# Both joins of a block's running sums in one burst of an attention kernel, instead of one in each of two

## The chip, the cores and the metric

The kernel runs on one core of one Trainium2 chip. The metric is the device time of one launch in microseconds (us): 1815.76 us, the median of three runs (1815.04 to 1822.94). The engines are named as in the profile: PE is TensorE's matmuls and PEld its weight loads, DVE is VectorE, ACT is ScalarE, POOL is GpSimd, SP is SyncE, which here issues DMAs.

## The reference, cut to what matters

```python
# x: (4, 512, 48, 48); 8 heads of d = 64 channels; t = 48 * 48 = 2304 tokens
hn  = group_norm(x, 32 groups) * scale + bias
qkv = einsum('oc,bchw->bohw', qkv_w, hn) + qkv_b        # then cast to float16
w   = softmax(einsum('bhct,bhcs->bhts', q * s, k * s), axis=-1)   # s = 64 ** -0.25
a   = einsum('bhts,bhcs->bhct', w, v)                   # float32
out = x + einsum('oc,bchw->bohw', proj_w, a) + proj_b
```

## The kernel before, in words

The attention is worked through in 16 pairs `g` of heads (4 images of 4 pairs; two heads side by side, 64 rows each). A pair's 2304 queries are cut into five blocks `j`: four of 512 queries and one of 256. So there are 80 blocks. For each block the 2304 keys are taken in bursts of three steps (`BURST = 3`); a block of 512 has six bursts, one of 256 has three. All bursts of all blocks stand in one list, `stream`, 432 entries long, and the loop over `n` at the end of `fast_path` goes through it. It writes every engine's queue by hand; no scheduler reorders it, and each engine works its own queue in order.

In the turn of burst `n` the loop writes, in this order:

- for a block whose last burst was `n - 3`: `add_up` (L1268), matmuls of the block's accumulator `acc` with a column of ones, which give the sums of the exponentials in the bank `sl`, and `rows` (L1284), DVE's copy of them out of the bank;
- `scores` of burst `n`: six matmuls (L1188) into three banks `ps`, and three exponentials on ACT (L1195) into the tile `p`;
- `add` of burst `n - 1`: on DVE, the burst's 128x3072 exponentials are added into `acc` (L1242). A block's first burst needs no addition, so the turn that handles it has none;
- `values` of burst `n - 2`: the matmuls `av<-p,v` (L1213), and, for a block's last burst, ACT's copy of the result to `avx` (L1222). The bank `av` is the one that `sl` takes over (`ps_av`, one buffer);
- `fill`: pieces of other work that are kept in the list `beside`: projections of q, k and v for later pairs and of the output for earlier ones (L840, L988, L717, L1092). A piece is a chain of matmuls into the one bank of `ps_w` and its evacuation on DVE (L868, L881, L727, L996, L1119). How many pieces a turn takes is set by a count of their costs and not by time;
- `join` at the end of the turn.

At a block's end `acc` holds three parts of 128x1024 (one for each step of a burst). `join(g, j, r)` adds part `r` to part 0 on DVE (L1247), so that `add_up` has one part to multiply by the ones. A block has two joins, `r = 1` and `r = 2`. With `e` the block's last burst, `r = 1` is written at the end of the turn `e + 1`, which also adds the exponentials of `e`, and `r = 2` at the end of the turn `e + 2`. The `add` of that turn is that of burst `e + 1`, the next block's first, so it adds nothing. `add_up` follows at the start of the turn `e + 3`. The last two blocks of the last pair don't join; 78 blocks do, with 156 joins.

POOL forms sums of x and of weights for the projections (L797, L775 to L778), multiplies `avx` by the inverse sums (L1337) and issues a DMA of the result (L1344).

Of the kernel before, what the change touches and what calls it, by code (L numbers as in the profile page):

```python
# [32 lines left out]
BURST = 3  # L33
# [434 lines left out]
def fast_path(  # L468
# [599 lines left out]
    def fetch(b, j):  # L1068

        o, n = QBLOCKS[j]  # L1070
        t = work.tile([P, NC, QB], F16, tag="attl", bufs=1, name=f"attl_{b}_{j}")
        pairs = NC - 1 if b == B - 1 else NC
        nc.sync.dma_start(
            t[:, :pairs, :n],
            atd[b].rearrange("(c p) t -> p c t", p=P)[:, :pairs, o : o + n],
        )
        fetched[b, j] = t
        fetch_at[b, j] = now[0]
# [89 lines left out]
    stream = []  # L1168
# [7 lines left out]
    def scores(u):  # L1176
        g, j, k, _ = u
        o, n = QBLOCKS[j]
        per = QB // n
        qt, kt = qk[g]  # L1180
        pt = ppool.tile([P, BURST, 2, QB], F16, tag="p", name=f"p_{g}_{j}_{k}")
        for r in range(BURST):
            ps = ps_s.tile([P, 2, QB], F32, tag="ps", name=f"ps_{g}_{j}_{k}_{r}")
            for a in range(per):
                i = (k * BURST + r) * per + a
                for h in range(2):
                    rows = slice(h * D, (h + 1) * D)
                    nc.tensor.matmul(  # L1188
                        ps[:, h, a * n : (a + 1) * n],
                        kt[rows, bass.ts(i, P)],  # L1190
                        qt[rows, o : o + n],
                        start=True,
                        stop=True,
                    )
            nc.scalar.activation(pt[:, r], ps, AF.Exp)  # L1195
        pts[u] = pt
# [27 lines left out]
    def add(u):  # L1224

        g, j, k, last = u
        pt = pts[u]
        if k == 0:
            acc[g, j] = [pt]
            return  # L1230
        if j >= NQ - 2 and g == NG - 1 and (last or j == NQ - 1):
            acc[g, j].append(pt)
            return
        before = acc[g, j][0]
        if k == 1:
            acc[g, j] = [
                work.tile(
                    [P, BURST, 2, QB], F16, tag="acc", bufs=1, name=f"acc_{g}_{j}"
                )
            ]  # L1240
        t = acc[g, j][0]
        nc.vector.tensor_tensor(t, before, pt, ALU.add)  # L1242

    def join(g, j, r):

        t = acc[g, j][0]
        nc.vector.tensor_tensor(t[:, 0], t[:, 0], t[:, r], ALU.add)  # L1247
        if r == BURST - 1:
            acc[g, j] = [t[:, :1]]

    def add_up(g, j, bank=None, more=False):


        o, n = QBLOCKS[j]
        per = QB // n
        sl = bank
        if bank is None:
            sl = ps_av.tile([P, QB], F32, tag="av", name=f"sl_{g}_{j}")
        steps = [
            (t, r, a)  # L1260
            for t in acc.pop((g, j))
            for r in range(t.shape[1])
            for a in range(per)
        ]
        for i, (t, r, a) in enumerate(steps):
            for h in range(2):
                lo = h * D
                nc.tensor.matmul(  # L1268
                    sl[lo : lo + D, :n],
                    ones16,  # L1270
                    t[:, r, h, a * n : (a + 1) * n],
                    start=(i == 0 and (g, j) not in open_sums),
                    stop=(i == len(steps) - 1 and not more),
                )
        if more:
            acc[g, j] = []
            open_sums.add((g, j))
        return sl

    def rows(g, j, sl):  # L1280

        o, n = QBLOCKS[j]
        sx = work.tile([P, QB], F32, tag="rows", name=f"slx_{g}_{j}")
        nc.vector.tensor_copy(sx[:, :n], sl[:, :n])  # L1284
        sm = small.tile([P, 2, QB // P], F32, tag="sums", name=f"sums_{g}_{j}")
        for h in range(2):
            nc.sync.dma_start(sm[:, h, : n // P], sx[h * D : h * D + 1, :n])
        sums[g, j] = sm
        return sx
# [9 lines left out]
    def check_sums(g, j):  # L1299
        n = QBLOCKS[j][1]  # L1300
        sm = sums[g, j][:, :, : n // P]
        ok = fine.rearrange("p (h i) -> p h i", h=2)[:, :, : n // P]
        for op, limit in ((ALU.is_ge, SUM_MIN), (ALU.is_le, SUM_MAX)):
            t = small.tile([P, 2, QB // P], F32, tag="in", name=f"in_{g}_{j}")
            t = t[:, :, : n // P]
            nc.gpsimd.tensor_scalar(t, sm, limit, None, op)  # L1306
            nc.gpsimd.tensor_tensor(ok, ok, t, ALU.mult)
# [278 lines left out]
    def pace(n):  # L1586

        rate, work = 0.0, 0.0
        for p in beside:
            us, need = p[0], p[6]  # L1590
            work += us
            left = min(need * per_pair, len(stream) - 4) - n
            rate = max(rate, work / max(left, 1))
        credit[0] = min(credit[0] + rate, 4.0)

    def fill(n, tasks_too=True):

        idle = beside and beside[0][4] and not beside[0][4]()  # L1600
        if ended(n - 1):
            room = 1.1 if idle else 0.0
        elif ended(n - BEHIND - 1):
            room = 1.1 if idle else 0.5
        else:
            room = 2.4 if idle else 0.8
        if tasks_too:
            do_tasks(room)
        closed = False
        while beside:  # L1610
            us, _, first, last, when, after = beside[0][:6]
            if after > n or (first and closed) or (when and not when()):
                break
            if us > 0.1 and credit[0] < us / 2:
                break
            issue()
            closed = closed or last
        if tasks_too:

            turn = next((p[7] for p in beside if len(p) > 7), None)  # L1620
            if turn is not None:
                prepare(turn + 1, 2)

    def wanted(g):

        while any(p[6] <= g for p in beside):
            while loads:
                loads.popleft()[1]()
            while tasks:
                tasks.popleft()[2]()  # L1630
            issue()
            credit[0] = max(credit[0], 0.0)

    ended = lambda n: 0 <= n < len(stream) and stream[n][3]
# [5 lines left out]
    def block_at(n):  # L1640

        return stream[n][:2] if ended(n) and n not in soon else None

    def joined(n):
        g, j = stream[n][:2]
        return not (g == NG - 1 and j >= NQ - 2)

    for n in range(end):
        now[0] = n
        while loads and loads[0][0] <= n:  # L1650
            loads.popleft()[1]()
        while fetches and fetches[0][0] <= n:
            fetch(*fetches.pop(0)[1:])
        summed = block_at(n - BEHIND - 1)
        pace(n)
        if summed:
            rows(*summed, add_up(*summed))
        wanted(stream[n][0])
        scores(stream[n])
        if n > 0:  # L1660
            add(stream[n - 1])
        if summed:

            fill(n)
        if n >= BEHIND:
            values(stream[n - BEHIND])
        if block_at(n - BEHIND - 2):
            check_sums(*block_at(n - BEHIND - 2))
        if block_at(n - BEHIND - 3):
            spread(*block_at(n - BEHIND - 3))  # L1670

        for late in (4, 5):
            found = block_at(n - BEHIND - late)
            if found and late == (4 if found[0] == NG - 1 else 5):
                divide(*found)
        if not summed:
            fill(n)

        if block_at(n - BEHIND - 2):
            invert(*block_at(n - BEHIND - 2))  # L1680
        for r in range(1, BURST):
            if ended(n - r) and joined(n - r):
                join(*stream[n - r][:2], r)
        if n - BEHIND in soon:
            g, j = stream[n - BEHIND][:2]
            sx = rows(g, j, add_up(g, j))
            if n - BEHIND == soon[1]:
                divide_here(g, j, sx, avx[g, j], nc.gpsimd)
        if n - BEHIND - 1 == soon[0]:
            check_sums(g, j)  # L1690
            invert(g, j)
        if n - BEHIND - 2 == soon[0]:
            spread(g, j)
            divide(g, j)
    g, b, j = NG - 1, B - 1, NQ - 1
    n = QBLOCKS[j][1]
# [99 lines left out]
```

## Time and profile before

| | |
|---|---|
| median of three runs | 1815.76 us (1815.04 to 1822.94) |
| the profiled execution | 1824.22 us, of which its instructions span 1822.5 us |
| busy: PE, DVE, ACT, POOL | 1603.8, 1284.5, 1341.7, 828.1 us |
| share of the span | 88%, 70%, 74%, 45% |
| mean granted clock of PE | 0.965 |
| joins (L1247) | 156, 163.2 us, mean 1046 ns |
| `sl` (L1268) | 192 matmuls, 35.3 us, and 151.6 us of idle PE before them |

In a row of groups stand line, engine, operation, the output and inputs by the program's names, the shapes and the count; behind the bar the busy time in us and the mean of one in ns; behind the second bar the idle time of that engine just before, and what ended it. A row of the timeline begins with start and length in us and ends with the idle time before it in brackets. A row of stretches begins with start, end and length, then gives for each engine the busy time and the count, and ends with PE's granted clock, the busy share of the DMA engines and GB/s; a `sum` row adds up such stretches.

### The profile page before, as it was taken

What the parts mean: (1) busy time and instruction counts of PE and PEld (TensorE: products, weight loads), DVE (VectorE), ACT (ScalarE), POOL (GpSimd) and SP (SyncE); (2) the same over time, 40 slices, a digit from 0 to 9 for tenths busy, and PEclk for the clock granted to TensorE, in tenths of its full rate; (3) what the DMA queues carried; (4) which work ended last, traced back from release to release, by engine and by line L of the source; (5) the groups of instructions that cost most, each with busy time, mean ns of one, the idle gap of its engine ahead of it and who ended that gap; (6) DMA issues with size and microseconds to landing.
All of it is one profiled execution on the core that took longest, in us unless ns stands there. A gap on an engine that the chain in (4) does not pass through costs nothing. (4 is left out here: it accounts for less than half of the span.)

```text
span 1822.5 us, 32530 instructions
## 1 busy us (share of the span) xinstructions
PE 1603.8 (88%) x12940; PEld 823.4 (45%) x12940; DVE 1284.5 (70%) x1553; ACT 1341.7 (74%) x1537; POOL 828.1 (45%) x1037
## 2 busy tenths in 40 slices
PE   6979898899989889989888999988989999889885
PEld 2634444344444444544444444444444444444443
DVE  5287677966767668796677767779777766776564
ACT  3267676677887778877777878787778778878783
POOL 2164652645664452264456445316456644552111
PEclk9999999999999999999999999999999999999898
DMA  6002020000100014610010002352100010223423
GB/s 202 1 10 62 17 72 15 20 19 17 30 22 21 16 63 134 170 42 23 22 30 23 19 15 65 102 183 60 24 27 23 25 22 17 68 72 118 134 86 106
DMA packets 108197, 100.07 MB, mean 55 GB/s; under 512 B 52372, under 2 KB 72084, under 8 KB 108036
## 3 DMA queue, kind: packets, MB, share of 16 engines
q1 hardware_dynamic: 102644, 87.20, 16.8%
q0 software_dynamic: 3488, 8.86, 1.5%
q8 instruction: 104, 1.70, 0.4%
q10 hardware_dynamic: 1904, 1.84, 0.3%
q14 instruction: 57, 0.47, 0.1%
HBM read 69.55 MB, written 28.01 MB: 54 GB/s over the span
## 5 line engine op out<-in xcount | busy, mean ns | idle before, releaser
L1195 ACT ACTIVATE p<-ps 128x1024 f16<-128x1024 f32 x1296 | 1232.1, 1026 | 439.1 <-PE ps L1188 370.3
L1242 DVE TENSOR_TENSOR acc<-acc,p 128x3072 f16<-128x3072 f16 x270 | 508.3, 1883 | 26.4 <-ACT p L1195 26.1
L1188 PE MATMUL ps<-q,k 64*128 64x512 f16 (+1 forms) x2880 | 372.7, 369 | 10.3 <-ACT p L1195 9.5
L1213 PE MATMUL av<-p,v 128*64 128x512 f16 (+1 forms) x2880 | 363.7, 366 | 0.1
L797 POOL TENSOR_TENSOR t<-x,t 128x256 f32<-128x256 f32 x240 | 205.0, 875 | 224.2 <-PE p L840 223.6
L988 PE MATMUL pv<-wqkv,x 128*64 128x256 f32 x2304 | 279.2, 391 | 6.4 <-DVE k L727 4.5
L1306 POOL TENSOR_SCALAR in<-sums 128x8 f32<-128x8 f32 (+1 forms) x158 | 89.4, 566 | 400.3 <-DMA sums<-slx 393.0
L1213 PEld LDWEIGHTS <-v 128*64 128x64 f16 x2880 | 132.8, 110 | 199.7 <-issue 151.1
L988 PEld LDWEIGHTS pv<-wqkv,x 128*64 128x64 f32 x2304 | 166.8, 141 | 104.7 <-issue 21.3
L1337 POOL TENSOR_TENSOR att<-avx,ib 128x512 f16<-128x512 f32 (+1 forms) x78 | 115.4, 1480 | 216.6 <-DMA ib<-row 197.7
L1188 PEld LDWEIGHTS <-k 64*128 64x128 f16 x2880 | 110.0, 96 | 220.2 <-issue 172.9
L840 PE MATMUL p<-t,s 128*64 128x256 f32 x1440 | 180.8, 388 | 3.5 <-DVE q L868 2.4
L1268 PE MATMUL sl<-acc,ones 128*64 128x512 f16 (+1 forms) x192 | 35.3, 393 | 151.6 <-DVE acc L1247 141.9
L1247 DVE TENSOR_TENSOR acc<-acc 128x1024 f16<-128x1024 f16 x156 | 163.2, 1046 | 0.7
L1242 DVE TENSOR_TENSOR acc<-p,p 128x3072 f16<-128x3072 f16 x79 | 150.0, 1899 | 0.0
L996 DVE TENSOR_TENSOR v<-pv,bv 128x512 f16<-128x512 f32 x72 | 49.7, 691 | 133.0 <-PE pv L988 133.0
L797 POOL TENSOR_TENSOR t<-x 128x256 f32<-128x256 f32 x120 | 130.4, 1107 | 22.6 <-PE p L840 22.4
L1092 PE MATMUL pr<-a,whi 128*128 128x512 f32 (+1 forms) x312 | 126.2, 412 | 10.0 <-ACT a L1064 4.8
L840 PEld LDWEIGHTS p<-t,s 128*64 128x64 f32 x1440 | 101.8, 140 | 66.9 <-issue 9.1
L797 POOL TENSOR_TENSOR t<-x,x 128x256 f32<-128x256 f32 x120 | 126.0, 1070 | 0.5 <-DVE x L668 0.4
L840 PE MATMUL p<-x,wqkv 128*64 128x256 f32 x960 | 121.7, 398 | 4.3 <-DVE v L996 2.8
L1092 PE MATMUL pr<-a,wlo 128*128 128x512 f32 (+1 forms) x312 | 117.5, 384 | 0.0
(90 smaller groups left out, 1326.5 us busy)
## 6 DMA issues: line engine op xcount, KB each, us to landing
r<-x_dram SPq DMA_DIRECT2D x72, 256.0 KB, 3.4
out_dram<-r SPq DMA_DIRECT2D x69, 256.0 KB, 2.3
ib<-row SPq DMA_DIRECT2D x126, 128.0 KB, 3.0
x<-x_dram SPq DMA_DIRECT2D x62, 256.0 KB, 5.1
attd<-att POOLq DMA_DIRECT2D x60, 128.0 KB, 2.2
attl<-attd SPq DMA_DIRECT2D x12, 512.0 KB, 4.2
x<-x_dram SPq DMA_DIRECT2D x16, 128.0 KB, 4.6
sums<-slx SPq DMA_DIRECT2D x128, 2.0 KB, 2.1
```

Of the source, the lines that this page charges most:

```text
L797: nc.gpsimd.tensor_tensor(t[:, c], ins[0][c], ins[1][c], ALU.subtract)
L840: nc.tensor.matmul(to[lo : lo + D, :], w[:, c, lo : lo + D], xs[c], start=(c == 0), stop=(c == 1),)
L988: nc.tensor.matmul(pw[0][lo : lo + D, a, :], hn[b, c, i * P // QB][:, at + lo : at + lo + D], wqkv[:, c, 2 * C + half * C // 2 :][:, : C / ...
L996: nc.vector.tensor_tensor(vv[b, half][:, i : i + 2, :], pw[0], bv[:, cols].unsqueeze(1).to_broadcast((P, 2, C // 2)), ALU.add,)
L1092: nc.tensor.matmul(ps[:, :n], w[:, c, bass.ts(m, P)], at32[b, j, c], start=(i == 0), stop=(i == len(steps) - 1),)
L1188: nc.tensor.matmul(ps[:, h, a * n : (a + 1) * n], kt[rows, bass.ts(i, P)], qt[rows, o : o + n], start=True, stop=True,)
L1195: nc.scalar.activation(pt[:, r], ps, AF.Exp)
L1213: nc.tensor.matmul(av[0][lo : lo + D, :n], vv[b, pr // 2][:, i, pr % 2 * P + lo : pr % 2 * P + lo + D], pt[:, r, h, a * n : (a + 1) * n], ...
L1242: nc.vector.tensor_tensor(t, before, pt, ALU.add)
L1247: nc.vector.tensor_tensor(t[:, 0], t[:, 0], t[:, r], ALU.add)
L1306: nc.gpsimd.tensor_scalar(t, sm, limit, None, op)
L1337: nc.gpsimd.tensor_tensor(to, avx.pop((g, j))[:, :n], ibs.pop((g, j))[:, :n], ALU.mult)
```

## The change

Both joins of a block are written at the end of the turn `e + 1`, the second directly behind the first; the turn `e + 2` has none. The sums are the same, in the same order.

```diff
         if block_at(n - BEHIND - 2):
             invert(*block_at(n - BEHIND - 2))
-        for r in range(1, BURST):
-            if ended(n - r) and joined(n - r):
-                join(*stream[n - r][:2], r)
+        if ended(n - 1) and joined(n - 1):
+            for r in range(1, BURST):
+                join(*stream[n - 1][:2], r)
         if n - BEHIND in soon:
```

On DVE's queue, around the end of pair 7's block 2, this stood before (`acc_2` is the block's accumulator, `t1q` and `q` the evacuation of the chain in the turn `e + 1`, `u2q` and `u3k` that in the turn `e + 2`, `slx` the copy of the sums):

```order
L1242 TENSOR_TENSOR acc_2_9043<-acc_2_9043,p_2_5_9139 128x3072
L881 TENSOR_SCALAR t1q_0_9202<-p_9_0_9193,bq 128x256
L868 SCALAR_TENSOR_TENSOR q_9191<-p_9_0_9193,t1q_0_9202 128x256
L1247 TENSOR_TENSOR acc_2_9043<-acc_2_9043 128x1024
L868 SCALAR_TENSOR_TENSOR u2q_0_9238<-p_9_0_9227,t1q_0_9202 128x256
L868 SCALAR_TENSOR_TENSOR u3k_0_9240<-p_9_0_9227,u2q_0_9238 128x256
L1247 TENSOR_TENSOR acc_2_9043<-acc_2_9043 128x1024
L1284 COPY slx_2_9246<-sl_2_9243 128x512
```

And this stands there now:

```order
L1242 TENSOR_TENSOR acc_2_9043<-acc_2_9043,p_2_5_9139 128x3072
L881 TENSOR_SCALAR t1q_0_9202<-p_9_0_9193,bq 128x256
L868 SCALAR_TENSOR_TENSOR q_9191<-p_9_0_9193,t1q_0_9202 128x256
L1247 TENSOR_TENSOR acc_2_9043<-acc_2_9043 128x1024 x2
L868 SCALAR_TENSOR_TENSOR u2q_0_9239<-p_9_0_9228,t1q_0_9202 128x256
L868 SCALAR_TENSOR_TENSOR u3k_0_9241<-p_9_0_9228,u2q_0_9239 128x256
L1284 COPY slx_2_9246<-sl_2_9243 128x512
```

The second join has moved ahead of the evacuation of the turn `e + 2`; nothing else changed places. On PE's queue the instructions stand in the same order as before. The chain in the turn `e + 3` (L840, behind `sl` and the six score matmuls) is where its waits differ; before, its rows and the two ahead of them were (`p` is the chain's bank, `ps` the scores; brackets name the semaphores waited for):

```order
L1188 LDWEIGHTS k_6424
L1188 MATMUL ps_3_2_2_9260<-q_6423,k_6424 128x512
L840 MATMUL p_9_0_9267<-t_9_0_8914,s_9_8906 64x256 [waits PE_49]
L840 MATMUL p_9_0_9267<-t_9_0_8914,s_9_8906 64x256 x3
L840 MATMUL p_9_0_9267<-x_2_0_6682,s_9_8909 64x256 x2
```

On PE's queue at the same place they now are:

```order
L1188 LDWEIGHTS k_6424
L1188 MATMUL ps_3_2_2_9260<-q_6423,k_6424 128x512
L840 MATMUL p_9_0_9267<-t_9_0_8914,s_9_8906 64x256 [waits DVE_49,PE_49]
L840 MATMUL p_9_0_9267<-t_9_0_8914,s_9_8906 64x256 x3
L840 MATMUL p_9_0_9267<-x_2_0_6683,s_9_8909 64x256 x2
```

The chain waits for DVE now, that is for the evacuation (`u3k`) of the bank that it writes; before, `sl` had already waited for a join that stood behind that evacuation.

## The prediction

> **What bounds the kernel now.** I read the waits of TensorE first, then the groups by line, then one block end on the timeline, then stretches behind every block end. In a row of waits stand the total, the number of waits and the longest.
>
> ```profile
> span 1822.5 us, 32530 instructions
> PE sl L1268 <- DVE acc L1247: 141.9, 69, 6.7
> PE sl L1268 <- ACT avx L1222: 9.7, 10, 2.2
> PE ps L1188 <- ACT p L1195: 9.5, 21, 0.5
> PE p L840 <- POOL t L797: 2.9, 1, 2.9
> ACT p L1195 <- PE ps L1188: 370.3, 300, 45.9
> L1247 DVE TENSOR_TENSOR acc<-acc 128x1024 f16<-128x1024 f16 x156 | 163.2, 1046 | 0.7
> ```
>
> TensorE hardly ever waits for ScalarE's exponentials (9.5 us) while ScalarE waits 370.3 us for scores, so TensorE sets the pace. Its one large wait is at `sl`, the matmuls that sum a block's accumulator: 141.9 us behind the joins (L1247). This block end (pair 7, block 2) shows why; the three fences are DVE, TensorE and ScalarE, with start, length and, in brackets, the idle time before.
>
> ```profile
> 916.67 0.42 DVE L868 SCALAR_TENSOR_TENSOR q<-p,t1q 128x256 f16<-128x256 f32 x1
> 917.01 0.68 DVE L1247 TENSOR_TENSOR acc<-acc 128x1024 f16<-128x1024 f16 x1
> 919.40 0.42 DVE L868 SCALAR_TENSOR_TENSOR u2q<-p,t1q 128x256 f32<-128x256 f32 x1 [1.71 <-PE p L840]
> 919.86 0.42 DVE L868 SCALAR_TENSOR_TENSOR u3k<-p,u2q 128x256 f32<-128x256 f32 x1
> 920.20 0.68 DVE L1247 TENSOR_TENSOR acc<-acc 128x1024 f16<-128x1024 f16 x1
> ```
>
> ```profile
> 917.46 1.89 PE L840 MATMUL p<-t,s 128*64 128x256 f32 x16
> 920.93 0.41 PE L1268 MATMUL sl<-acc,ones 128*64 128x512 f16 x2 [1.59 <-DVE acc L1247]
> 921.27 0.82 PE L1188 MATMUL ps<-q,k 64*128 64x512 f16 x6
> 924.55 0.82 PE L1188 MATMUL ps<-q,k 64*128 64x512 f16 x6
> ```
>
> ```profile
> 919.19 0.61 ACT L1222 COPY avx<-av 128x512 f32<-128x512 f32 x1
> 921.71 1.02 ACT L1195 ACTIVATE p<-ps 128x1024 f16<-128x1024 f32 x1 [1.91 <-PE ps L1188]
> ```
>
> The second join stands on DVE's queue behind `u2q` and `u3k`, the evacuation of the projection chain that TensorE itself has just finished at 919.35. So TensorE finishes the chain, DVE evacuates it for 0.8 us, joins for 0.68 us, and only then may `sl` start. DVE had been idle from 917.69 to 919.40: 1.71 us, in which a join of 0.68 us fits.
>
> **The change, part by part.** No arithmetic is added or removed: 78 second joins move one burst forward, to right behind the first join. SP's and POOL's queues issue the same instructions in the same order; the joins issue no DMA.
>
> (a) The wait at `sl`. With the second join at 917.70 to 918.38, what ends last is no longer DVE: it is `avx`, ScalarE's copy out of the one bank that `sl` takes over, ending at 919.80. I therefore cut out, for the 78 blocks that join, the stretch from the latest of three ends (TensorE's last matmul before `sl`; `avx`; first join plus the second join's length of this trace) to the start of `sl`. The first row is the sum of the whole waits of the 78, then that of the cut stretches.
>
> ```profile
> sum 149.85, PE 0.21 PEld 0.71 DVE 135.92 ACT 40.50 POOL 65.82; mean PE 0.00 PEld 0.01 DVE 1.74 ACT 0.52 POOL 0.84
> sum 88.20, PE 0.10 PEld 0.17 DVE 83.07 ACT 6.00 POOL 29.00; mean PE 0.00 PEld 0.00 DVE 1.20 ACT 0.09 POOL 0.42
> sum 100.03, PE 0.10 PEld 0.17 DVE 94.72 ACT 6.00 POOL 39.03; mean PE 0.00 PEld 0.00 DVE 1.37 ACT 0.09 POOL 0.57
> sum 83.10, PE 0.09 PEld 0.16 DVE 78.20 ACT 5.94 POOL 26.88; mean PE 0.00 PEld 0.00 DVE 1.22 ACT 0.09 POOL 0.42
> ```
>
> So 88.2 us of 149.9. In 60 blocks `avx` governs, in 13 the join, in 5 TensorE's own end. The third row takes every second join at the undisturbed 0.68 us: 100.0, the upper end. The fourth holds those that would start inside a POOL run behind a POOL DMA until that run ends (next fence): 83.1, less 4.2 for five blocks that would then come later: 78.9, the lower end. That `sl` really follows `avx` at once is seen where today's two joins already stand back to back:
>
> ```profile
> 867.60 1.41 DVE L1247 TENSOR_TENSOR acc<-acc 128x1024 f16<-128x1024 f16 x2
> 869.79 0.61 ACT L1222 COPY avx<-av 128x512 f32<-128x512 f32 x1
> 870.45 0.41 PE L1268 MATMUL sl<-acc,ones 128*64 128x512 f16 x2 [0.50 <-ACT avx L1222]
> 871.27 2.85 ACT L1195 ACTIVATE p<-ps 128x1024 f16<-128x1024 f32 x3 [0.87 <-ACT avx L1222]
> ```
>
> ScalarE there still idles 0.87 us against 1.91 above, so it gains as much as TensorE and doesn't become the limit.
>
> (b) What holds a join. The first two rows are the joins of one block on DVE, the next three POOL at that time, the last is the longest join.
>
> ```profile
> 388.25 1.15 DVE L1247 TENSOR_TENSOR acc<-acc 128x1024 f16<-128x1024 f16 x1
> 389.44 3.67 DVE L1247 TENSOR_TENSOR acc<-acc 128x1024 f16<-128x1024 f16 x1
> 389.15 0.61 POOL L1344 DMA_DIRECT2D attd<-att  x1 [0.30 <-POOL att L1337]
> 389.79 1.41 POOL L797 TENSOR_TENSOR t<-x,x 128x256 f32<-128x256 f32 x2
> 391.15 1.39 POOL L797 TENSOR_TENSOR t<-x,t 128x256 f32<-128x256 f32 x2
> 891.15 5.96 DVE L1247 TENSOR_TENSOR acc<-acc 128x1024 f16<-128x1024 f16 x1
> ```
>
> The second was held until POOL's run behind its DMA ended; 12 of the 156 joins of today last over 2.5 us, the longest 5.96. I keep the present share, which the 88.2 contains. The other way round, a POOL instruction can be held by a join that now runs earlier; TensorE waits for POOL's sums 2.9 us in all, so I cost that at nothing. The Trainium skill ("SBUF — State Buffer", section "Who interferes with whom") says that a VectorE instruction with two SBUF inputs contends with GpSimd's reads and that whoever starts first has the shared ports for its whole instruction. By that a join waits for one POOL instruction at most, and the sum would lie near the 100.0 end; the row disagrees, since the join sat through four, and the row decides.
>
> (c) The evacuation of the second burst now stands behind the second join. In the block shown the join ends at 918.38 and the evacuation can't start before 919.40, so it costs nothing; the cover is those 1.0 us, and a join held longer pushes the evacuation. The next chain on TensorE waits for that evacuation by a semaphore of its own now. With `sl` at 919.85 that chain starts after `sl` and six score matmuls, 1.09 us later (920.93 to 922.02 today), at 920.94; `u3k` ends at 920.28. Nothing, with 0.66 us to spare.
>
> (d) TensorE's clock. The rows are the 3.62 us behind `sl` in two blocks, with the granted clock before the last two numbers, and TensorE's instructions in the slower one.
>
> ```profile
> 920.93:924.55 3.62, 3.62 (x30) 1.74 (x31) 2.85 (x4) 2.84 (x4) 1.35 (x2) 1.00 0.04 1
> 1085.53:1089.15 3.62, 3.62 (x20) 1.63 (x22) 2.36 (x2) 2.79 (x3) 3.62 (x4) 0.60 0.06 6
> 1085.53 0.41 PE L1268 MATMUL sl<-acc,ones 128*64 128x512 f16 x2 [1.96 <-DVE acc L1247]
> 1090.79 0.82 PE L1188 MATMUL ps<-q,k 64*128 64x512 f16 x6
> ```
>
> From `sl` to the next burst's scores it is 3.62 us at full clock and 5.26 us here: 1.64 us lost. Over all 78, the low clock follows 23 of the 31 waits of 1.8 us and more, and of the 47 shorter ones only one, inside a low stretch that had begun before the wait. With the waits of (a) shortened, 12 of the 23 fall under 1.8 us (16 at its upper end, 10 at its lower): 12 × 1.64 = 19.7 us more (16.4 to 26.2). The Trainium skill ("TensorE: Matmul & The Clock Gate", section "What's actually happening") has the clock halve after an idle window of about 3.4 us. By that only the 8 waits over 3.4 us would count and the term would be at most 13.1 us; here waits of 1.9 us were enough.
>
> **The sum.** 88.2 + 19.7 = 107.9 us off the profiled execution's 1824.22: 1716.3. The median of the runs lies 8.46 us below that execution, as much as five low-clock stretches (8.46 / 1.64). If it had 18 of them behind waits and not 23, (d) is 12/23 × 18 × 1.64 = 15.4, the gain 103.6 and the time 1815.76 − 103.6 = **1712 us**.
>
> **The rivals.** *The clock doesn't care* (0.18): low stretches come as often as before, wherever TensorE pauses. For it: 8 of the 31 waits of 1.8 us and more weren't followed by one. Then 88.2 alone: 1728, or 1737 with the lower end.
>
> ```profile
> sum 267.00, PE 125.84 PEld 69.41 DVE 152.67 ACT 157.10 POOL 105.85; mean PE 1.61 PEld 0.89 DVE 1.96 ACT 2.01 POOL 1.36
> ```
>
> That is the time from the end of the first join to the start of `sl`, over the 78 blocks: 3.42 us each.
>
> *POOL holds the pair* (0.13): POOL's run is released by the same TensorE chain and starts about when the second join now does. If a third of the blocks (26) meets it, these lose their 1.13 us of (a) (88.2/78), a third of (d), about 6, and with a hold like the 3.67 us of 389.44 come 0.25 us later than today (3.67 − 3.42), 6.5 in all. 103.6 − 29.4 − 6 − 6.5 = 62: 1754. Against it: where the joins already are a pair, few are held.
>
> *Slower* (0.05): the same place with the longest hold. A second join of 5.96 us, the length of 891.15, puts `sl`, the evacuation and the next chain 2.5 us later than today, against a gain of 1.38 us (107.9/78) in other blocks; it decides from 28 blocks of 78 on. With 40 blocks: 40 × 2.5 − 38 × 1.38 = 48 us more, 1864. Against it: one join in 156 is held that long today.
>
> *No change* (0.04): TensorE's next wait gives all of it back, at ScalarE or a late DVE evacuation. The 9.5 us in 21 waits for `p` speak against it: 1811 to 1820.
>
> **The numbers.** My forecast with its own bounds has 0.60: 1815.76 − 126.2 = 1690 to 1815.76 − 95.3 = 1720. The range takes in the clock rival and the POOL rival up to 1758; slower and no change are left out, with 0.09. Faster by over 0.5% (9 us, about the spread of the three runs) is 0.60 + 0.18 + 0.13 = 0.91.
>
> **What would show it.** Right: TensorE's wait at `sl` behind the joins falls from 141.9 us to under 30 and that behind `avx` rises to some 30 to 45 us in about 60 waits; few low-clock stretches behind `sl`; ScalarE's idle time there about 0.9 us. Wrong: joins of mean length well over 1.05 us, POOL's runs under them, or new TensorE waits for L868 or L996.

## The result, and the profile after

The changed kernel takes 1731.75 us (median of four runs, 1725.04 to 1733.21) against 1816.31 us before (1815.04 to 1822.94): a ratio of 0.952, 95% interval 0.9486 to 0.9554. The forecast was 1712, with bounds of its own of 1690 to 1720; the stated range, which takes in two rivals, was 1690 to 1758. The profiled execution took 1731.0 us, with a mean granted clock of 0.974 against 0.965.

The page of the changed kernel, its span, the busy times and the group of the joins:

```profile
span 1729.3 us, 32531 instructions
PE 1587.3 (92%) x12940; PEld 823.5 (48%) x12940; DVE 1286.5 (74%) x1553; ACT 1340.8 (78%) x1537; POOL 856.3 (50%) x1037
...
L1247 DVE TENSOR_TENSOR acc<-acc 128x1024 f16<-128x1024 f16 x156 | 167.0, 1071 | 2.9
```

TensorE's waits in it (total, number, longest):

```profile
PE sl L1268 <- DVE acc L1247: 34.4, 17, 4.5
PE sl L1268 <- ACT avx L1222: 31.4, 55, 2.2
...
PE ps L1188 <- ACT p L1195: 13.2, 28, 1.4
PE p L840 <- POOL t L797: 7.0, 2, 4.1
```

The joins do as much work as before (167.0 us against 163.2), but TensorE waits for them 34.4 us and not 141.9. In 55 blocks it waits for `avx`. This is the end of pair 7's block 2 on the timeline, a fence each for DVE, TensorE and ScalarE.

```profile
875.84 1.41 DVE L1247 TENSOR_TENSOR acc<-acc 128x1024 f16<-128x1024 f16 x2
878.22 0.42 DVE L868 SCALAR_TENSOR_TENSOR u2q<-p,t1q 128x256 f32<-128x256 f32 x1 [0.98 <-PE p L840]
```

```profile
876.28 1.89 PE L840 MATMUL p<-t,s 128*64 128x256 f32 x16
878.67 0.41 PE L1268 MATMUL sl<-acc,ones 128*64 128x512 f16 x2 [0.50 <-ACT avx L1222]
...
882.29 0.82 PE L1188 MATMUL ps<-q,k 64*128 64x512 f16 x6
```

```profile
878.02 0.60 ACT L1222 COPY avx<-av 128x512 f32<-128x512 f32 x1
879.44 1.02 ACT L1195 ACTIVATE p<-ps 128x1024 f16<-128x1024 f32 x1 [0.82 <-PE ps L1188]
```

Both joins are over 0.97 us before the evacuation can begin, `sl` waits 0.50 us for `avx` where it waited 1.59 us for the join, and ScalarE idles 0.82 us where it idled 1.91. From `sl` to the second scores it is 3.62 us, as before.

TensorE's account in the two profiled executions, whose spans differ by 93.2 us: its idle time before `sl`, both releasers together, fell from 151.6 to 65.7 us (85.9 less); its busy time fell by 16.5 us with the same 12940 matmuls, because fewer of them ran at the low clock (29 low stretches before, 18 now, counted in the granted clock); its idle time elsewhere rose by about 9 us. 85.9 + 16.5 − 9 is 93.4.

### The profile page after: what moved, and what is told of

The parts are those of the page before. It is cut to its first block, busy times and chain, and to the rows that moved or that the text cites. A ratio compares the mean times of both kernels' runs of the same rounds, so it can differ in the third digit from the quotient of the medians.

```text
span 1729.3 us, 32531 instructions
## 1 busy us (share of the span) xinstructions
PE 1587.3 (92%) x12940; PEld 823.5 (48%) x12940; DVE 1286.5 (74%) x1553; ACT 1340.8 (78%) x1537; POOL 856.3 (50%) x1037
## 5 line engine op out<-in xcount | busy, mean ns | idle before, releaser
L1188 PE MATMUL ps<-q,k 64*128 64x512 f16 (+1 forms) x2880 | 368.5, 364 | 13.9 <-ACT p L1195 13.2
L797 POOL TENSOR_TENSOR t<-x,t 128x256 f32<-128x256 f32 x240 | 224.4, 955 | 187.7 <-PE p L840 187.1
L1306 POOL TENSOR_SCALAR in<-sums 128x8 f32<-128x8 f32 (+1 forms) x158 | 97.3, 616 | 345.7 <-DMA sums<-slx 338.1
L1337 POOL TENSOR_TENSOR att<-avx,ib 128x512 f16<-128x512 f32 (+1 forms) x78 | 121.7, 1560 | 198.2 <-DMA ib<-row 167.7
L988 PEld LDWEIGHTS pv<-wqkv,x 128*64 128x64 f32 x2304 | 167.0, 140 | 105.0 <-issue 20.9
L840 PE MATMUL p<-t,s 128*64 128x256 f32 x1440 | 184.4, 393 | 8.6 <-POOL t L797 7.0
L1247 DVE TENSOR_TENSOR acc<-acc 128x1024 f16<-128x1024 f16 x156 | 167.0, 1071 | 2.9
L1242 DVE TENSOR_TENSOR acc<-p,p 128x3072 f16<-128x3072 f16 x79 | 156.6, 1982 | 0.0
L840 PEld LDWEIGHTS p<-t,s 128*64 128x64 f32 x1440 | 102.7, 141 | 72.8 <-issue 10.1
L797 POOL TENSOR_TENSOR t<-x,x 128x256 f32<-128x256 f32 x120 | 119.9, 1019 | 1.2 <-DVE x L668 1.1
L840 PE MATMUL p<-x,wqkv 128*64 128x256 f32 x960 | 115.4, 382 | 3.6 <-DVE k L727 2.4
L1119 DVE SCALAR_TENSOR_TENSOR r<-pr,bproj,r 128x512 f32<-128x512 f32 (+1 forms) x80 | 55.0, 695 | 68.5 <-PE pr L1092 64.1
```

The lines of the kernel that those rows point to most:

```text
L797: nc.gpsimd.tensor_tensor(t[:, c], ins[0][c], ins[1][c], ALU.subtract)
L840: nc.tensor.matmul(to[lo : lo + D, :], w[:, c, lo : lo + D], xs[c], start=(c == 0), stop=(c == 1),)
L988: nc.tensor.matmul(pw[0][lo : lo + D, a, :], hn[b, c, i * P // QB][:, at + lo : at + lo + D], wqkv[:, c, 2 * C + half * C // 2 :][:, : C / ...
L1119: nc.vector.scalar_tensor_tensor(xt[:, i], places[i], bias, xt[:, i], ALU.add, ALU.add)
L1188: nc.tensor.matmul(ps[:, h, a * n : (a + 1) * n], kt[rows, bass.ts(i, P)], qt[rows, o : o + n], start=True, stop=True,)
L1337: nc.gpsimd.tensor_tensor(to, avx.pop((g, j))[:, :n], ibs.pop((g, j))[:, :n], ALU.mult)
```

## The experiments

Each time stands beside a kernel before that ran on the same chip: 1820.01 us for the first four, 1818.6 for the last three. Low-clock stretches are counted in the granted clock of each profiled execution.

**The opposite: both joins in the turn e + 2.**

```diff
-        if ended(n - 1) and joined(n - 1):
+        if ended(n - 2) and joined(n - 2):
             for r in range(1, BURST):
-                join(*stream[n - 1][:2], r)
+                join(*stream[n - 2][:2], r)
```

> Both joins at the end of the turn e + 2, none in e + 1. Theory (the join counts where it stands behind the evacuation that follows the chain TensorE has just finished): the first join now stands there too and adds its 0.68 to 1.05 us to each of 78 waits, 53 to 82 us; most waits of 1.4 to 1.6 us then exceed 1.8 us, so that some 45 to 58 low-clock stretches follow instead of 23, another 35 to 57 us: 1900 to 1955 us. Rival (only DVE's total work counts, the place doesn't matter): 1816 us, as before. Rival (place counts, clock doesn't follow the waits): 1869 to 1898 us.

Measured: 1914.72 us, ratio 1.0511 (1.0473 to 1.0549). The row of TensorE's wait, then one block end on the timelines of DVE and of TensorE:

```profile
PE sl L1268 <- DVE acc L1247: 183.4, 68, 7.0
```

```profile
958.85 0.42 DVE L868 SCALAR_TENSOR_TENSOR u3k<-p,u2q 128x256 f32<-128x256 f32 x1
959.19 1.41 DVE L1247 TENSOR_TENSOR acc<-acc 128x1024 f16<-128x1024 f16 x2
```

```profile
960.65 0.64 PE L1268 MATMUL sl<-acc,ones 128*64 128x512 f16 x2 [2.31 <-DVE acc L1247]
```

DVE's total work is the same; only the place is another, and it costs 95 us. The wait before `sl` grew less than expected (195.3 us in all against 151.6, 44 more); fewer joins are held by POOL at the new place (7 over 2.5 us against 12). The low stretches rose from 29 to 55, 48 of them behind the 69 waits of 1.8 us and more; that carries the rest: TensorE's busy time is 49.4 us up (1653.2 against 1603.8).

**The clock alone: the kernel before, with TensorE kept busy in part of its wait.**

```diff
+    def warm(u):
+        ...
+        for _ in range(4):
+            nc.tensor.matmul(
+                ps[:, 0, :], kt[:, 0:P], qt[:, 0:QB], start=True, stop=True
+            )
+        ahead_ps.append(ps)
...
         if summed:
+            warm(stream[n])
             rows(*summed, add_up(*summed))
```

> The kernel before with its joins where they were, and four added 128x512 matmuls on TensorE ahead of sl at each block end, into the score bank that the next scores overwrite. They take 0.85 us of the wait and shorten no dependency, so sl starts when it did. Clock theory (a pause of 1.8 us or more is what brings the low-clock stretch): the waits left are 0.85 us shorter, 12 to 15 of the 23 low stretches behind them go, 20 to 25 us less, and the eight blocks that wait only 0.5 us lose 0.35 us each: 1794 to 1799 us. Rival (low stretches come whatever TensorE does): 1816 to 1819 us and as many low stretches as before.

Measured: 1795.8 us, ratio 0.9876 (0.9845 to 0.9907). The joins stand where they stood before, and `sl` still waits for them; on the timeline are the added matmuls (L1186) and `sl`.

```profile
907.24 1.04 PE L1186 MATMUL ps<-q,k 128*128 128x512 f16 x4
908.89 0.41 PE L1283 MATMUL sl<-acc,ones 128*64 128x512 f16 x2 [0.62 <-DVE acc L1262]
```

TensorE's wait in total, and the span with the mean granted clock:

```profile
PE sl L1283 <- DVE acc L1262: 75.1, 66, 5.7
```

```profile
core 0: 1794.3 us, clock 0.985
```

Work was added, nothing was shortened, and the kernel became 1.2% faster: the mean clock rose from 0.965 to 0.985 and the low stretches fell from 29 to 10. So the pause brings the low clock. More stretches went than the 12 to 15 expected, and the span fell by 28.2 us, 1.5 us for each of the 19, against the 1.64 of the prediction. The rival, that low stretches come whatever TensorE does, is out.

**What still holds joins: the DMA of the divided result on SP's queue.**

```diff
-            nc.gpsimd.dma_start(at, to)
+            nc.sync.dma_start(at, to)
```

> The changed kernel, with the DMA of the divided result (L1344) issued by SP's queue and not by POOL's. Theory (a join is held for a whole POOL run only behind POOL's own DMA): the 12 joins over 2.5 us fall to 0 to 2, the wait of sl for joins from 34.4 us to under 8, and with some 5 low-clock stretches fewer 1695 to 1710 us. Rival (any POOL run holds a join): 12 long joins stay, 1726 to 1735 us. Rival (SP's queue, which now waits for POOL's division, brings its loads late): over 1740 us.

Measured: 1676.03 us, ratio 0.9205 (0.9178 to 0.9232). In the changed kernel 13 joins lasted over 2.5 us. The longest pair in the changed kernel, on DVE's timeline, and POOL's run beside it:

```profile
647.40 7.02 DVE L1247 TENSOR_TENSOR acc<-acc 128x1024 f16<-128x1024 f16 x2
```

```profile
647.75 0.61 POOL L1344 DMA_DIRECT2D attd<-att  x1 [0.30 <-POOL att L1337]
648.38 1.42 POOL L797 TENSOR_TENSOR t<-x,t 128x256 f32<-128x256 f32 x2
...
652.48 1.39 POOL L797 TENSOR_TENSOR t<-x,t 128x256 f32<-128x256 f32 x2
```

The joins' durations (least, median and most in ns, then the first and last start), first in the changed kernel, then with the DMA on SP's queue:

```profile
L1247 DVE TENSOR_TENSOR acc<-acc x156: 639/692/6309, 106.1 to 1673.6; 128x1024 f16<-128x1024 f16 x156
```

```profile
L1247 DVE TENSOR_TENSOR acc<-acc x156: 637/693/1646, 105.8 to 1623.4; 128x1024 f16<-128x1024 f16 x156
```

And TensorE's waits before `sl` with it there:

```profile
PE sl L1268 <- ACT avx L1222: 36.7, 67, 2.2
...
PE sl L1268 <- DVE acc L1247: 4.6, 3, 3.5
```

No join is held over 1.65 us now, though POOL runs its sums as before (856.3 and 846.2 us busy): a long hold needs POOL's own DMA in the run. The trace of the changed kernel bears it out: there 52 joins start with over 1.5 us of an unbroken POOL run still ahead; the 13 long ones are all among the 30 whose run had POOL's DMA in it ahead of them, and the other 22 last 1.27 us at most. But 17 of those 30 weren't held either, and what decides between them stays open. The gain is 55.7 us and not the 20 to 35 expected. Of the 56.4 us by which the span fell, the wait at `sl` gave 23.4; low stretches fell from 18 to 8 and not by five, and TensorE's busy time by 19.0; its idle time elsewhere gave 7.7. Another 6.2 us have nothing to do with joins: they lie behind TensorE's last matmul (14.1 us before, 7.9 now). DVE is busy 43.5 us less (1243.0 against 1286.5) and the joins make up 35 of that.

**The next wait: `avx` ahead of the third exponential.**

```diff
-            nc.scalar.activation(pt[:, r], ps, AF.Exp)
+            if hold and r == BURST - 1:
+                held.append((pt[:, r], ps))
+            else:
+                nc.scalar.activation(pt[:, r], ps, AF.Exp)
...
-        scores(stream[n])
+        scores(stream[n], ended(n - BEHIND))
...
             values(stream[n - BEHIND])
+        while held:
+            nc.scalar.activation(*held.pop(), AF.Exp)
```

> The changed kernel, with ScalarE's copy avx ahead of the third exponential of the turn e + 2 and not behind it. Theory (avx is what sl now waits for in 55 blocks, 31.4 us): the copy ends some 1.0 us earlier, that wait falls to under 6 us, and the time by 20 to 28 us: 1703 to 1712 us. Rival (ScalarE is the bound there; the third exponential, 0.6 us later, holds up the next scores): 1728 to 1735 us with a new wait of TensorE for p.

Measured: 1700.94 us, ratio 0.9361 (0.9331 to 0.9392), a little better than expected. TensorE's waits, and one block end on the timelines of ScalarE (the exponential held back is L1673) and of TensorE:

```profile
PE sl L1273 <- DVE acc L1252: 36.2, 19, 4.5
PE ps L1190 <- ACT p L1200: 15.1, 31, 1.7
...
PE sl L1273 <- ACT avx L1227: 3.8, 4, 1.3
```

```profile
856.28 0.59 ACT L1227 COPY avx<-av 128x512 f32<-128x512 f32 x1
856.75 1.05 ACT L1673 ACTIVATE p<-ps 128x1024 f16<-128x1024 f32 x1
```

```profile
857.17 0.38 PE L1273 MATMUL sl<-acc,ones 128*64 128x512 f16 x2
```

The wait for `avx` is nearly gone (31.4 to 3.8 us) and `sl` starts without a pause; that for `p` rose by 1.9 us only. So `avx` was what ended last at the changed kernel's block ends, and ScalarE had room.

**The DMA without the change: the kernel before, DMA on SP's queue.** The edit is the same line as in the third experiment.

> The kernel before, joins in two turns as they were, with the DMA of the divided result on SP's queue. Theory (holds by POOL and the place of the second join are two separate costs): the 12 joins over 2.5 us go, which lengthened some 14 of the waits of sl by about 27 us in all, and about 8 low-clock stretches with them: 1770 to 1785 us; the other waits of 1.4 to 1.6 us stay and sl still waits for the join in about 69 blocks, some 110 us. Rival (the DMA's queue matters only once the joins stand together): 1810 to 1820 us.

Measured: 1769.59 us, ratio 0.9727 (0.9699 to 0.9755), just under the 1770 to 1785 expected. The join wait and the joins' durations:

```profile
PE sl L1268 <- DVE acc L1247: 117.8, 65, 5.7
```

```profile
L1247 DVE TENSOR_TENSOR acc<-acc x156: 639/683/1648, 105.8 to 1715.8; 128x1024 f16<-128x1024 f16 x156
```

Without held joins the wait behind the evacuation stays, in 65 blocks. The two costs are separate: 2.7% for the DMA alone (some 6 of its 49 us again behind TensorE's last matmul), 4.8% for the joins' place alone, 8.0% for both, where the product of the two would give 7.4%.

**Both further edits together.** The changed kernel with the DMA on SP's queue and `avx` early.

> The changed kernel with both: the DMA on SP's queue and avx ahead of the third exponential. Theory (they remove different waits, so they add): the 36.7 us in 67 waits of sl for avx fall to under 8, 1643 to 1652 us. Rival (with the joins freed ScalarE becomes the bound, and TensorE waits for p instead): 1662 to 1676 us, with waits for p well over 15 us.

Measured: 1646.11 us, ratio 0.9048 (0.9026 to 0.9069), the best of all; against the changed kernel 0.9048 / 0.952 = 0.950 by the two ratios, without an interval of its own. Its span, and TensorE's waits:

```profile
span 1642.1 us, 32524 instructions
```

```profile
PE ps L1190 <- ACT p L1200: 12.4, 29, 0.5
...
PE sl L1273 <- DVE acc L1252: 5.8, 8, 3.5
PE sl L1273 <- ACT avx L1227: 4.6, 4, 1.3
```

The pause at the block end is all but gone: 10.6 us of idle TensorE before `sl` against 151.6 at first. ScalarE did not become the bound.

**Earlier still: both joins ahead of the evacuation of the turn e + 1.**

```diff
             add(stream[n - 1])
+        if ended(n - 1) and joined(n - 1):
+            for r in range(1, BURST):
+                join(*stream[n - 1][:2], r)
         if summed:
...
-        if ended(n - 1) and joined(n - 1):
-            for r in range(1, BURST):
-                join(*stream[n - 1][:2], r)
```

> As the kernel with both, and the two joins ahead of the evacuation of the turn e + 1 and not behind it. Theory (behind the evacuation the joins already end before sl can start; ahead of it they push that evacuation by 1.4 us, and the chain of the turn e + 2 waits for it): 5 to 40 us slower than the kernel with both. Rival (an earlier join is always better): faster than it by some us.

Measured: 1698.86 us, ratio 0.9339 (0.9315 to 0.9362), 52.8 us slower than the kernel with both edits, more than the 5 to 40 expected. Two of TensorE's waits, then one place on the timelines of DVE and of TensorE:

```profile
PE p L840 <- DVE k L868: 21.5, 18, 2.1
...
PE p L840 <- DVE q L868: 7.1, 9, 1.9
```

```profile
868.89 1.42 DVE L1252 TENSOR_TENSOR acc<-acc 128x1024 f16<-128x1024 f16 x2
...
871.02 0.41 DVE L868 SCALAR_TENSOR_TENSOR k<-p,u3k 128x256 f16<-128x256 f32 x1
```

```profile
871.58 1.95 PE L840 MATMUL p<-t,wqkv 128*64 128x256 f32 x16 [1.39 <-DVE k L868]
```

The joins wait here for nothing and push the evacuation, for which the next chain on TensorE waits 1.39 us. Its idle time is 43 us more (118.7 against 75.7); the profiled span is 44.3 us longer. The other 8 us of the medians go for the most part with the clock, by estimate: this kernel's median execution had 0.989 where the profiled one had 0.993, and 0.004 of 1690 us is about 7. So the place right behind the evacuation of `e + 1` isn't better because it is earlier: it is the gap in which DVE would have waited for TensorE.

## Why the prediction was right, and where its sizes were off

The mechanism of (a) and (d) was right, but the number was not within the forecast's own bounds: 1731.75 us lies above 1690 to 1720, in the part of the range that was added for the rivals. It lies next to what the first rival gives, 1728 (the clock doesn't care), and that is chance. The runs refute this rival: low stretches fell from 29 to 18 here, and to 10 by the added matmuls alone. The clock did give its 16.5 us, and waits that had been put at nothing, with the step to the median, took about as much back.

The forecast's own sum is held against the profiled execution: 107.9 us off 1824.22, and 93.2 us of span came.

*Term (a), the wait at `sl`: right.* 88.2 us forecast, 85.9 measured. The three ends that were compared for it are those that decide: `avx` in 55 blocks with 31.4 us (forecast 60 with 30 to 45), the join in 17 with 34.4 us (forecast 13, and under 30 us).

*Term (d), the clock: right in kind, slightly large.* 19.7 us (12 stretches) forecast; 11 stretches fewer and 16.5 us of busy time measured. In the changed kernel a low stretch began behind 10 of the 15 waits of 1.8 us and more and behind none of the 57 shorter ones; the experiment with added matmuls shows the cause. The Trainium skill ("TensorE: Matmul & The Clock Gate", section "What's actually happening") ties the low clock to an idle window of about 3.4 us; the trace agrees that idle time brings it, but the 1.96 us of the block end at 1085.53 were enough, and there the measurement decides.

The length of a pause is only half of it. In the clock records of all nine traces the low stretches begin on a fixed grid with steps of 3.413 us, and TensorE's idle share of a step at full clock settles the clock of the next step. In the kernel before, a low step followed none of the 455 steps that were idle for less than half, 1 of the 6 idle for 50 to 55%, 12 of the 13 idle for 55 to 60%, and all 15 above that. These are grid steps around two pauses of the same 1.96 us (1083.57 to 1085.53 and 1631.66 to 1633.62):

```profile
1082.87:1086.28 3.41, 1.45 (x14) 0.49 (x12) 2.13 (x6) 1.55 (x3) 3.33 (x5) 1.00 0.01 2
1086.28:1089.69 3.41, 3.41 (x18) 1.67 (x16) 2.55 (x3) 2.86 (x3) 3.41 (x4) 0.50 0.06 6
...
1629.01:1632.42 3.41, 2.65 (x24) 1.38 (x22) 1.46 (x4) 3.41 (x5) 0.86 (x2) 1.00 0.65 192
1632.42:1635.83 3.41, 2.21 (x13) 1.26 (x14) 2.91 (x5) 1.53 (x3) 0.00 (x0) 1.00 0.01 2
1635.83:1639.25 3.42, 3.42 (x27) 1.55 (x27) 2.95 (x3) 2.63 (x4) 1.70 (x2) 1.00 0.25 78
```

The first pause fell into one step, left it idle for 57%, and the next step ran at half clock; a border of the grid cut the second in two, no step was idle for over 35%, and the clock stayed. The 8 of 31 waits that the prediction counted for its rival are all of the second kind: no step around them was idle for over 52%.

*The waits put at nothing: mis-sized.* (b) put TensorE's wait for POOL's sums at nothing, because it was 2.9 us in all; (a) had ScalarE gain as much as TensorE and not become the limit. Some 9 us came back there: the wait for POOL rose from 2.9 to 7.0 us, that for `p` from 9.5 to 13.2, and smaller ones make up the rest. The evacuation, which (c) put at nothing, did cost nothing in its own wait, 0.2 us for `u3k` before and after. The largest single piece is in this row of the changed kernel's timeline:

```profile
329.01 3.68 PE L840 MATMUL p<-t,s 128*64 128x256 f32 x16 [4.07 <-POOL t L797]
```

TensorE reached that chain before POOL had its sums. No join runs on DVE between 318 and 333 us, so this isn't the case that (b) named, a join that holds POOL. The small wait for POOL that (b) took as proof of cover belonged to a TensorE that came later; it holds no longer when TensorE comes sooner.

*Step (b), held joins: the share stayed, as assumed* (12 before, 13 after over 2.5 us), and with it the rival of a third of the blocks held fell. But that POOL's DMA is what makes a run hold a join was only inferred there; the third experiment shows it. The Trainium skill ("SBUF — State Buffer", section "Who interferes with whom") has the ports go to whoever starts first, for one instruction; the pair of 7.02 us shows a hold over a run of POOL's DMA and eight instructions, and the measurement decides.

*The step from the execution to the median: its premise isn't borne out.* The sum gave 1716.3 for the profiled execution. I then took that execution's surplus of 8.46 us over the median for five low stretches, and so 103.6 off the median, for 1712. One low stretch lowers an execution's mean clock by 0.0009 (half of 3.41 us in 1822), so five lower it by nearly 0.005. The experiments came with the clock of twenty more executions of the kernel before: the four within 1.5 us of the median had 0.964 to 0.967, against 0.965 in the profiled one. So two or three stretches at most are in the surplus; what the rest was stays open. By the medians the gain is 84.0 us (1815.76 − 1731.75), 19.6 less than 103.6: 14.7 from the sum and 4.9 from this step. Of the 14.7, the waits put at nothing are about 9, (d) 3.2 and (a) 2.3.

## What to carry to other kernels

When an in-order engine serves another, ask at each of its queued instructions what the instruction ahead of it waits for. Work whose inputs are ready, but which stands behind the evacuation of what the waiting engine has only just produced, belongs ahead of that evacuation, in the gap where its engine would wait; one place further ahead it costs again. After such an edit the next-latest end is named by the same block end (here `avx`, then the joins held by POOL), and each can be tried by itself.

## What the hardware showed that was not expected

- A pause of TensorE of 1.8 to 2 us is enough for a 3.4 us stretch at half clock behind it, if it falls into one step of the clock's 3.413 us grid: in the kernel before a low stretch followed 23 of 31 pauses of 1.8 us and more and 1 of 47 shorter ones; in the first experiment 48 of 69 and 1 of 10. In the nine traces together a low step followed none of the 4140 full-clock steps that were idle for less than half, and all 115 that were idle for 60% and more. Four idle-time matmuls at each block end made the kernel 1.2% faster.
- A DVE addition of two float16 inputs in SBUF that takes 0.68 us alone took up to 6.31 us while POOL worked off a run that began with a DMA of its own queue. With that DMA on SP's queue and POOL's sums unchanged, the longest was 1.65 us, and the kernel before gained 2.7% from that line alone.
